# A four-layer metaformer on one core: zero products on TensorE, one broadcast of B written twice, and an accumulation moved behind a scan

## The chip, the cores and the metric

The kernel runs on one core of a Trainium2 chip. The metric is the device time of one execution in microseconds (us), as the median of the executions timed. The engines are called by the profile's names: PE (TensorE, matmuls; PEld is its weight load), DVE (VectorE), ACT (ScalarE), POOL (GpSimd) and SP (SyncE, which here only issues transfers). Each engine works through its own instructions in order and waits on semaphores for the others.

## The reference

The input is x of shape (4, 64, 64, 96). Four layers are applied, each a normalisation over the 96 channels, a mixer and a residual add, and then a small feed-forward block on quantised values with its own residual add. Layer 0's mixer is a gated recurrence. Layers 1 to 3 have a selective scan as mixer, and it is there that the change lies. Cut to what matters, for one direction k, channel d and state n:

```
xs = silu(conv3x3(x @ in_proj))        # 192 channels, 4096 positions, 4 directions
dts, Bs, Cs = split(x_proj @ xs)       # Bs, Cs: 16 states
delta = softplus(dt_proj @ dts + bias)
def step(h, inp):                      # along the 4096 positions
    u_l, dl, b_l, c_l = inp
    dA = exp(dl[..., None] * A)
    h = dA * h + (dl * u_l)[..., None] * b_l[:, :, None, :]
    y = einsum('bkdn,bkn->bkd', h, c_l)
    return (h, y)
y = ys + Ds * u
```

The four directions are added, normalised, gated with silu(z) and projected out.

## The kernel before

Layer 0 is done first for all four images by `gated`. Then `scans` goes through twelve stages, layers 1 to 3 of four images each. A stage has 24 items: two directions `d`, four segments of 1024 positions and three chunks of 128 rows (a row is a channel of one of the two scan orders). An item has 16 tiles, one for each state n. That makes 12 x 24 x 16 = 4608 tiles of 128 x 1024 floats, and the loop takes them in pairs: one step `j` of the loop at the end of `scans` handles tiles a = 2j and b = 2j + 1, so there are 2304 steps.

For a tile k these are the operations, by the helpers' names:

- `decays(k)`: ACT computes da = exp(delta * A).
- `b_rows(k)`: PE spreads row n of B over the 128 rows, by two bf16 matmuls of 512 columns with a matrix `sel` of ones and zeros, into a tile `bc` of PSUM.
- `times_b(k)`: DVE multiplies `bc` in place by `du`.
- `scan(k)`: DVE runs h = da * h + bc along the 1024 positions.
- `c_rows(k)`: SP issues two transfers that spread row n of C into a tile `c` of SBUF (six buffers).
- `times_c(k)`: POOL multiplies h into `c`.
- `accumulate(k)`: PE adds `c` to the open sum `acc` of the item, by four float32 matmuls of 64 x 512 which the profile lists as eight rows. The sum stands open over the 16 tiles.

The tile `bc` comes from `wide()`, which asks a pool of two PSUM buffers for a new tile at each call. With `acc` (two banks) and the two banks of the side work this fills PSUM's eight banks. A buffer is given to a new tile by the scheduler once every instruction that touches the tile before in it has been placed; the new tile's writer then waits for those instructions.

Each engine's instructions stand in the order in which the Python code issues them (the class `InOrder` chains them), so the order written in the loop is the order on the engine. In a step DVE runs `times_b(a)`, `times_b(b)`, `scan(a)`, `scan(b)`. PE runs `accumulate(a - 4)`, `accumulate(b - 4)`, then the side work, then `b_rows(a + 2)` and `b_rows(b + 2)` for the step that follows.

The side work is what lies between two scans: joining directions, the output projection, the feed-forward block, the next layer's input projection and convolution, and preparing the next item's delta. It is written as generators, and `beside` pumps them twice in a step, once after `times_b(a)` and once after `scan(a)`. `pe.columns` counts the columns that PE has been given so far, a float32 column as four; `slot` and the jobs' `share` and `rate` use that count to spread the side work over the steps. At an item's step 6 (`n == 13`) the preparation of the next item is drained to its end, and near the end of a stage the job for the next stage is drained as well.

Of the kernel before, what the change touches and what calls it, by code (L numbers as in the profile page):

```python
# [12 lines left out]
BF16 = mybir.dt.bfloat16  # L13
# [13 lines left out]
MM = 512  # L27
# [10 lines left out]
NB3 = 96  # L38
# [35 lines left out]
    return n / (max(1, 128 // max(rows, 32)) * max(1, 128 // max(cols, 32)))  # L74


PACE = (2.0, 1600), (2.2, 1800), (2.6, 2000)


# [37 lines left out]
def metaformer(ctx: ExitStack, tc: tile.TileContext, x, l0_ab, l0_rest, ssm, ffn, out):  # L117
    nc = tc.nc
    pe, act, dve, pool, sp = (
        InOrder(tc, e) for e in (nc.tensor, nc.scalar, nc.vector, nc.gpsimd, nc.sync)  # L120
    )
# [6 lines left out]
    def sb(bufs, tag, shape, dtype=F32):  # L128
        return pools[bufs].tile(shape, dtype, tag=tag, name=tag)

    def const(name, shape, dtype=F32):
        return pools[1].tile(shape, dtype, name=name)
# [3 lines left out]
    def wide():  # L136
        return wides[0].tile([128, T], F32, tag="bc", name="bc")
# [11 lines left out]
    def settle():  # L149
        banks["free"] += banks["back"]  # L150
        banks["back"] = 0
# [20 lines left out]
    def drain(chain, others=lambda: None, until=lambda: False):  # L172

        while chain is not None and not chain.done and not until():
            if not pump(chain):
                others()
            settle()
# [16 lines left out]
    sel = const("sel", [NB3, NS, 128], BF16)  # L194
    for n in range(NS):
        for k in range(2):
            at = NS * k + n
            dve.tensor_copy(
                sel[:, n, 64 * k : 64 * k + 64], mod32[:, at : at + 1].to_broadcast([NB3, 64])
            )  # L200

    fold = const("fold", [128, 32])
    dve.tensor_tensor(fold, ident[:, 0:32], ident[:, 32:64], ALU.add)
# [9 lines left out]
    for layer in range(4):  # L213
# [8 lines left out]
        b = const(f"b_{layer}", [128, 3 + C])  # L222
# [538 lines left out]
    def slot():  # L761

        load["now"] = max(0, min(load["now"], 4 * load["most"]) - load["most"])
# [102 lines left out]
    def prepare_chunk(item):  # L866

        w, sg = weights[item.layer].w, item.sg
        i = 3 * item.d + item.chunk
        bias = w[:, W_DTB + i : W_DTB + i + 1]  # L870
        f = w[NB3 : NB3 + 2 * R, W_IN + 128 * i : W_IN + 128 * (i + 1)]


        delta, du = sb(2, "delta", [128, T]), sb(2, "du", [128, T])
        for k in range(2):
            cols = slice(k * MM, (k + 1) * MM)
            ps = bank("dt_proj")
            pe.matmul(ps, f, sg.rows[NB3 : NB3 + 2 * R, cols], start=True, stop=True)
            yield
            act.activation(delta[:, cols], ps, AF.Identity, bias=bias)  # L880
            release()
            yield k == 0
        act.activation(delta, delta, AF.Softplus)
        exp_and_ln()
        yield
        yield
        pool.tensor_tensor(du, delta, sg.us[item.chunk], ALU.mult)
        item.delta, item.du = delta, du
# [13 lines left out]
    def scans(stages, jobs, pac):  # L902
# [16 lines left out]
        tiles = [(i, n) for i in items for n in range(NS)]  # L919
        last = len(tiles) - 1  # L920
# [10 lines left out]
        def c_rows(k):  # L931
            i, n = tiles[k]
            c = live[k, "c"] = sb(6, "c", [128, T])
            for half in range(2):
                row = NS * half + n
                sp.dma_start(
                    out=c[64 * half : 64 * half + 64],
                    in_=i.sg.cs[row : row + 1, :].to_broadcast([64, T]),
                )
# [7 lines left out]
        def b_rows(k):  # L947
            i, n = tiles[k]
            b = live[k, "b"] = wide()
            for half in range(2):  # L950
                cols = slice(half * MM, (half + 1) * MM)
                pe.matmul(
                    b[:, cols], sel[:, n, :], i.sg.bs[:, cols], start=True, stop=True
                )
# [31 lines left out]
        def add_quarters(i, v, lhs, start, stop):  # L986

            for k in range(2):
                for j in range(2):
                    p = slice(64 * j, 64 * j + 64)  # L990
                    o = 64 * (j ^ k)
                    pe.matmul(
                        i.acc[o : o + 64, j * MM : (j + 1) * MM],
                        lhs[p],
                        v[p, k * MM : (k + 1) * MM],
                        start=start,
                        stop=stop,
                        tile_position=(64 * j, o),
                    )

        def accumulate(k):
            i, n = tiles[k]
            h = live.pop((k, "c"))
            if n == 0:
                i.acc = pac.tile([128, T], F32, tag="acc", name="acc")
                if i.d == 0:
                    add_quarters(i, i.sg.us[i.chunk], weights[i.layer].skip[:, i.chunk, :], True, False)
                else:
                    add_quarters(i, i.yf, stacked, True, False)
            add_quarters(i, h, stacked, False, n == NS - 1)  # L1010

        def take(i):
            i.y = sb(2, "y", [128, T])
            act.copy(i.y, i.acc)
# [27 lines left out]
        for j in range(len(tiles) // 2 + 2):  # L1042
            q, m = divmod(j, half)
            a, b = 2 * j, 2 * j + 1
            on = b <= last
            if on:
                item = items[q]
                nxt = at(q + 1)
                if m == 0:
                    if q % per == 0:  # L1050
                        item.im.y = dram.tile([3, 128, L], F32, tag="y", name="y")
                        working += jobs[q // per]
                    chain = None
                if m == 2 and nxt is not None:
                    if item.chunk == 2:
                        drain(segment, work, lambda: nxt.sg.steps)
                    chain = Chain(prepare_chunk(nxt), True)
                if item.chunk == 1 and m == 1 and at(q + 2) is not None:
                    if q % per == per - 2:
                        for job in jobs[q // per][:1]:  # L1060
                            while not job.done:
                                job.step()
                                settle()
                    segment = Chain(next_segment(items[q + 2 : q + 5]))
                if m == 4 and nxt is not None:
                    start(nxt)
                    if nxt.d == 1:
                        nxt.yf = sb(2, "y", [128, T])
                        t = slice(nxt.seg * T, (nxt.seg + 1) * T)
                        sp.dma_start(out=nxt.yf, in_=nxt.im.y[nxt.chunk, :, t])  # L1070

            def beside(n):
                slot()
                pumped(chain)
                pumped(segment)
                if n == 13:
                    drain(chain, work)
                    if item.chunk == 2:
                        drain(segment, work)
                work(True)  # L1080
                settle()

            if on:
                decays(b)
            for k in (a - 2, b - 2):
                if 0 <= k <= last:
                    carry(k)
            if a + 2 <= last:
                decays(a + 2)
            if 0 <= b - 2 <= last:  # L1090
                times_c(b - 2)
                del live[a - 2, "h"], live[b - 2, "h"]
            for k in (a - 4, b - 4):
                if 0 <= k <= last:
                    accumulate(k)
                if k + 6 <= last:
                    c_rows(k + 6)
            if on:
                times_b(a)
            beside(2 * m)  # L1100
            if on:
                times_b(b)
                scan(a)
            beside(2 * m + 1)
            if a + 2 <= last:
                b_rows(a + 2)
            if on:
                times_c(a)
                scan(b)
            if b + 2 <= last:  # L1110
                b_rows(b + 2)
            if m == 1 and q >= 1:
                take(items[q - 1])
                store(items[q - 1])
# [241 lines left out]
    with tc.tile_pool(name="pbig", bufs=2, space=bass.MemoryType.PSUM) as wides_pool:  # L1356
# [5 lines left out]
        for at in range(len(stages)):  # L1362
            jobs.append([])
            if at + 1 < len(stages):
                im, layer = stages[at + 1]
                jobs[-1].append(Job(between(im, layer - 1), *PACE[layer > 1]))

            for im in {10: images[:2], 11: images[2:3]}.get(at, ()):
                jobs[-1].append(Job(between(im, 3, im.dst), *PACE[2]))
        with tc.tile_pool(name="pac", bufs=1, space=bass.MemoryType.PSUM) as pac:  # L1370
# [121 lines left out]
```

## Time and profile before

| what | value |
|---|---|
| median of three executions | 19407.92 us (19403.34 to 19430.67) |
| the profiled execution's own time | 19356.33 us |
| its span, first to last instruction | 19354.5 us |
| PE busy | 14811.6 us, 77% |
| ACT busy | 10683.2 us, 55% |
| POOL busy | 13500.1 us, 70% |
| scan, 128x1024, on DVE | 4608 instructions, mean 2331 ns |
| `times_b`, 128x1024, on DVE | 4608 instructions, mean 1216 ns |
| `times_c`, 128x1024, on POOL (other forms among them) | 4992 instructions, mean 2276 ns |
| `accumulate`'s matmuls, rows of 64x512 | 36864 rows, 6192.7 us busy |
| `b_rows`, rows of 96x512 bf16 | 9216 rows, 3171.1 us busy |
| mean granted TensorE clock | 0.823 |

The page counts an engine as busy while one of its instructions runs; matmuls overlap, so a group's busy time is less than rows times mean. "Idle before" in a row is the time that the engine stood idle just ahead of it, and the name behind the arrow is what ended that idle time. The granted clock is the share of TensorE's full clock that it was allowed in a stretch.

### The profile page before, as it was taken

How to read it: one execution, taken by the hardware profiler on the slowest of the kernel's cores; microseconds unless marked ns; L12 is line 12 of the kernel's file. 1: busy time of each engine (PE TensorE's matmuls, PEld its weight loads, DVE VectorE, ACT ScalarE, POOL GpSimd, SP SyncE). 2: the span in 40 equal slices, each digit the busy share in tenths (PEclk: the TensorE clock that was granted, in tenths of full speed). 3: DMA queues.
4: the chain of work that ended last, by engine and by line, in shares of the span. 5: the costliest groups of instructions: out<-in, count | busy, mean ns of one | idle time of the engine just before them, and what ended most of it. 6: DMA issues, size and time to landing. Idle time of an engine off the chain costs nothing.

```text
span 19354.5 us, 236828 instructions
## 1 busy us (share of the span) xinstructions
PE 14811.6 (77%) x75584; PEld 4774.9 (25%) x75584; DVE 17417.6 (90%) x13768; ACT 10683.2 (55%) x17977; POOL 13500.1 (70%) x9220
## 2 busy tenths in 40 slices
PE   8897776776777777777777777777777777777777
PEld 3332121221222222222222222222222222222224
DVE  7668999999999999999999999999999999998994
ACT  3444565565555565565565565565565565565554
POOL 3435777777777777777777777777777777777774
PEclk9898887887887787787887887787887887787876
DMA  2123676676677667667677677667667677677773
GB/s 54 49 60 99 171 189 171 173 189 169 177 191 179 174 179 182 174 180 186 173 181 182 173 182 180 170 180 183 173 180 182 173 180 182 172 182 177 180 179 92
DMA packets 1269928, 3193.12 MB, mean 165 GB/s; under 512 B 440336, under 2 KB 440560, under 8 KB 1262544
## 3 DMA queue, kind: packets, MB, share of 16 engines
q1 hardware_dynamic: 1268688, 3177.97, 64.7%
q8 instruction: 609, 9.98, 0.2%
q14 instruction: 631, 5.17, 0.1%
HBM read 2818.51 MB, written 308.28 MB: 162 GB/s over the span
## 4 chain that ended last, share of the span: by engine, by line
issue 35%; PE 22%; DVE 20%; ACT 6%; DMA 4%; POOL 3%; SPq 1%; POOLq 0%; DVEq 0%; ACTq 0%
DVE h L91 13%; PE acc L91 11%; DVE bc L91 5%; PE bc L91 4%; POOL c L91 2%; PE y_t L91 2%; ACT L91 2%; PE dt_proj L91 1%; DMA c<-cs 1%; ACT da L91 1%; ACT u L91 1%; PE out_proj L91 1%; DVE st L91 1%; SPq L91 1%; DMA u<-u 1%
## 5 line engine op out<-in xcount | busy, mean ns | idle before, releaser
L91 POOL TENSOR_TENSOR c<-h,c 128x1024 f32<-128x1024 f32 (+1 forms) x4992 | 11281.7, 2276 | 4576.5 <-DVE h L91 1847.5
L91 DVE TENSOR_TENSOR_SCAN h<-da,carry,bc 128x1024 f32<-128x1024 f32 x4608 | 10585.8, 2331 | 263.6 <-ACT da L91 205.4
L91 ACT ACTIVATE da<-delta,decay 128x1024 f32<-128x1024 f32 x4608 | 5262.1, 1146 | 2266.5 <-DVE h L91 2256.8
L91 PE MATMUL acc<-c,twice 64*64 64x512 f32 x36864 | 6192.7, 801 | 52.9 <-POOL c L91 52.9
L91 DVE TENSOR_TENSOR bc<-du,bc 128x1024 f32<-128x1024 f32 x4608 | 5475.3, 1216 | 737.2 <-PE bc L91 722.3
L91 PE MATMUL bc<-bs,sel 96*128 96x512 bf16 x9216 | 3171.1, 440 | 3619.7 <-DVE h L91 3518.2
L91 PEld LDWEIGHTS acc<-c,twice 64*64 64x64 f32 x36864 | 1550.1, 172 | 3485.6 <-issue 2661.7
L91 PEld LDWEIGHTS <-sel 96*128 96x128 bf16 x9216 | 639.4, 102 | 5978.4 <-DVE h L91 5470.6
L91 ACT ACTIVATE delta<-dt_proj,w 128x512 f32<-128x512 f32 x576 | 394.4, 685 | 1547.2 <-PE dt_proj L91 1546.0
L91 ACT COPY carry<-h 128x1 f32<-128x1 f32 x3456 | 580.0, 184 | 1080.5 <-DVE h L91 1076.2
L91 ACT ACT_TABLE_LOAD x857 | 1099.5, 1283 | 15.7 <-PEq L1485 0.7
L91 PE MATMUL conv<-pad,taps 64*64 64x256 f32 (+1 forms) x9216 | 781.8, 393 | 42.4 <-ACT u L91 33.3
L91 POOL TENSOR_TENSOR du<-delta,u 128x1024 f32<-128x1024 f32 x288 | 678.3, 2355 | 16.1 <-ACT delta L91 14.6
L91 PE MATMUL x_proj<-u,xp 128*108 128x512 f32 x1152 | 632.3, 660 | 62.3 <-DMA u<-u 34.5
L91 PE MATMUL dt_proj<-rows,w 12*128 12x512 f32 x1152 | 669.7, 662 | 3.7 <-ACT u L91 2.7
L91 ACT ACTIVATE c<-c,l_bias 128x512 f32<-128x512 f32 x384 | 263.8, 687 | 726.8 <-PE c L91 716.8
L91 PEld LDWEIGHTS conv<-pad,taps 64*64 64x64 f32 (+1 forms) x9216 | 430.4, 142 | 600.5 <-issue 387.7
L91 DVE TENSOR_TENSOR_SCAN h<-da,l_carry,bc 128x512 f32<-128x512 f32 x384 | 491.4, 1280 | 41.0 <-DVE bc L91 1.4
L91 POOL CAST hq<-ff_h 128x512 fp8e5<-128x512 f16 x384 | 233.3, 611 | 326.7 <-ACT ff_h L91 326.6
L91 PE MATMUL y_t<-ident,pad 128*128 128x128 f32 (+1 forms) x1536 | 401.8, 348 | 54.2 <-DMA pad<-y 46.8
L91 ACT COPY u<-conv 64x256 f32<-64x256 f32 x768 | 280.6, 365 | 241.7 <-PE conv L91 143.3
L91 PE MATMUL bc<-rows,u 96*128 96x512 f32 x768 | 391.8, 635 | 28.2 <-DVE h L91 27.5
(138 smaller groups left out, 11927.0 us busy)
## 6 DMA issues: line engine op xcount, KB each, us to landing
c<-cs SPq DMA_DIRECT2D x9216, 256.0 KB, 4.5
u<-u SPq DMA_DIRECT2D x288, 512.0 KB, 6.8
y<-y SPq DMA_DIRECT2D x1152, 128.0 KB, 4.2
y<-y SPq DMA_DIRECT2D x144, 512.0 KB, 6.4
xr<-x SPq DMA_DIRECT2D x224, 192.0 KB, 5.3
u<-u SPq DMA_DIRECT2D x288, 128.0 KB, 4.0
pad<-y SPq DMA_DIRECT2D x288, 128.0 KB, 5.8
z<-zl SPq DMA_DIRECT2D x96, 256.0 KB, 4.8
```

Of the source, the lines that this page charges most:

```text
L91: ins = f(*a, **k).ins
```

## The change

Three things are altered in the loop, all on PE and with it one transfer issue on SP:

- `accumulate(b - 4)` and `c_rows(b + 2)` move from the head of the step to a place behind `scan(a)`, the side work and `b_rows(a + 2)`.
- `b_rows(a + 2)` is called twice. Each call takes a new tile from `wide()`; the second takes the entry `live[a + 2, "b"]` over, and `times_b(a + 2)` reads that one. Nothing reads the first.
- Ahead of them `keep_busy` adds up to nine matmuls of 512 columns with `nothing`, a tile of zeros, as stationary operand, into the open sum of tile a - 4's item. Their number is (4608 less the columns that PE was given by the step's side work) / 512.

```diff
+FILL = 4608
...
+    nothing = const("nothing", [NB3, 128], BF16)
+    pool.memset(nothing, 0.0)
...
+        def keep_busy(i, n):
+
+            for j in range(n):
+                pe.matmul(
+                    i.acc[:, j % 2 * MM : (j % 2 + 1) * MM],
+                    nothing,
+                    sel[:, 0 : MM // 128, :],
+                    start=False,
+                    stop=False,
+                )
...
-            for k in (a - 4, b - 4):
-                if 0 <= k <= last:
-                    accumulate(k)
-                if k + 6 <= last:
-                    c_rows(k + 6)
+            if 0 <= a - 4 <= last:
+                accumulate(a - 4)
+            if a + 2 <= last:
+                c_rows(a + 2)
+            before = pe.columns
             if on:
                 times_b(a)
             beside(2 * m)
...
                 times_b(b)
                 scan(a)
             beside(2 * m + 1)
+            if 0 <= a - 4 <= last:
+                keep_busy(tiles[a - 4][0], max(0, FILL - int(pe.columns - before)) // MM)
             if a + 2 <= last:
-                b_rows(a + 2)
+                for _ in range(2):
+                    b_rows(a + 2)
+            if 0 <= b - 4 <= last:
+                accumulate(b - 4)
+            if b + 2 <= last:
+                c_rows(b + 2)
             if on:
                 times_c(a)
                 scan(b)
```

## The prediction

> **What bounds the kernel now.** I read the engines' shares first, then DVE's waits, then the timeline of a step without disturbance. The page's first part:
>
> ```profile
> PE 14811.6 (77%) x75584; PEld 4774.9 (25%) x75584; DVE 17417.6 (90%) x13768; ACT 10683.2 (55%) x17977; POOL 13500.1 (70%) x9220
> ```
>
> DVE is busy 90% of the span, no other engine over 77%. What little DVE waits, by the list of who waited for whom (total us, times, longest):
>
> ```profile
> DVE bc L91 <- PE bc L91: 722.3, 494, 17.9
> ...
> DVE h L91 <- ACT da L91: 205.4, 44, 18.0
> ```
>
> It waits for a broadcast in 494 of 2304 steps, 1.46 us each; in the other 79% PE is in time. One of those, in order of time (start, duration, what; in brackets idle time and its end):
>
> ```profile
> 2821.95 2.33 DVE L91 TENSOR_TENSOR bc<-du,bc 128x1024 f32<-128x1024 f32 x2
> 2822.06 0.19 ACT L91 COPY carry<-h 128x1 f32<-128x1 f32 x1 [1.01 <-DVE h L91]
> 2822.08 0.11 PEld L91 LDWEIGHTS <-sel 96*128 96x128 bf16 x2 [1.71 <-DVE h L91]
> 2822.09 0.61 PE L91 MATMUL bc<-bs,sel 96*128 96x512 bf16 x2 [1.22 <-DVE h L91]
> ...
> 2822.62 1.95 PE L91 MATMUL acc<-c,twice 64*64 64x512 f32 x16
> ...
> 2824.20 4.57 DVE L91 TENSOR_TENSOR_SCAN h<-da,carry,bc 128x1024 f32<-128x1024 f32 x2
> ```
>
> times_b(a) and times_b(b) start 1.13 us apart (2821.95 to 2824.20 for two), two scans follow, and the next pair starts at 2828.69: a step of 6.74 us that DVE alone sets. The broadcast at 2822.09 is tile b's: it waits for the end of scan(b), and times_b(a) covers it. Tile a's was written during scan(b). That half scan of lead is what keeps DVE supplied.
>
> **The second broadcast, and the buffer that it gets.** This decides the case. The first call of b_rows(a + 2) takes the buffer that scan(a) frees; for the second, the built program shows which of the two buffers the scheduler chose. PE's order in one step, with the semaphores waited for:
>
> ```
> Matmult bc_41866<-bs_40331,sel_95 128x512 [waits DVE_49]
> ...
> Ldweights sel_95 [waits DVE_49]
> Matmult bc_41869<-bs_40331,sel_95 128x512 [waits PE_49]
> ...
> Matmult acc_41838<-c_41728,twice_87 64x512 [waits DMAHW6_49,Pool_49]
> ...
> Matmult bc_41882<-bs_40331,sel_95 128x512 [waits PE_49]
> ```
>
> bc_41869, the copy that times_b(a + 2) reads, waits for DVE once more, and the count it waits for is that of scan(b): it was put into b's buffer, and b + 2 (bc_41882) into that of the unread copy. Counted over the program, 1849 of 2303 second copies are so placed ("crossed"); in 454 both copies share a's buffer. A crossed copy can't be written during scan(b). Right behind scan(b) DVE wants times_b(a + 2), so DVE stands still until the copy is there, and PE, in order, holds accumulate(b - 4) and b_rows(b + 2) behind it.
>
> **What a crossed step costs.** No step of the trace waits like this, so I build it from rows for a broadcast that DVE did wait for, at full clock and at half (start of the broadcast, then of times_b):
>
> ```profile
> 8007.72 1.04 PE L91 MATMUL bc<-bs,sel 96*128 96x512 bf16 x4
> 8008.36 1.23 DVE L91 TENSOR_TENSOR bc<-du,bc 128x1024 f32<-128x1024 f32 x1 [1.48 <-PE bc L91]
> ```
>
> ```profile
> 1860.85 1.89 PE L91 MATMUL bc<-bs,sel 96*128 96x512 bf16 x4
> ...
> 1861.92 1.23 DVE L91 TENSOR_TENSOR bc<-du,bc 128x1024 f32<-128x1024 f32 x1 [0.60 <-PE bc L91]
> ```
>
> So 0.64 us at full clock, 1.07 at half. Add 0.13 us, by which the broadcast's weights start after times_b would have (2821.95 to 2822.08): the first stall is 0.77 us, or 1.20.
>
> The second stall is at times_b(b + 2). Its broadcast follows the copy and accumulate(b - 4). At full clock accumulate starts 0.53 us behind the copy's start (2822.09 to 2822.62), takes half of 1.95 = 0.98, and 0.64 later times_b(b + 2) may run: 2.15. times_b(a + 2) started at 0.64 and frees DVE at 1.77. Stall 0.38. At half clock the rows are these:
>
> ```profile
> 8016.18 1.04 PE L91 MATMUL bc<-bs,sel 96*128 96x512 bf16 x2 [2.54 <-DVE h L91]
> ...
> 8017.15 3.69 PE L91 MATMUL acc<-c,twice 64*64 64x512 f32 x16
> ```
>
> 0.97 + 1.85 + 1.07 = 3.89 against 1.07 + 1.13 = 2.20: stall 1.69.
>
> Which clock? The granted clock, by stretches of 3.4 us (PE busy is the first figure after the stretch, the clock comes behind POOL):
>
> ```profile
> 2812.00:2815.40 3.40, 0.66 (x3) 0.17 (x4) 3.40 (x3) 1.30 (x3) 2.70 (x2) 1.00 0.79 213
> 2815.40:2818.80 3.40, 3.40 (x18) 0.94 (x22) 3.40 (x3) 1.64 (x3) 2.46 (x2) 0.53 0.28 70
> ```
>
> PE was busy 0.66 of 3.4 us, and in the next 3.4 us the clock was 0.53. Over the whole trace about a third of the broadcasts that start promptly behind scan(b) run at half clock, and half of the accumulates behind them. The fill evens PE's work out, but a crossed step still has a hole of 1.7 us ahead of every second copy (from the first copy's end to scan(b)'s end; before it was 1.22 to 1.63). I keep these shares: 0.77 + 0.43/3 = 0.91 and 0.38 + 1.31/2 = 1.04, together 1.95 us. Side work of DVE between the two times_b (their starts lie 1.29 us apart on average, not 1.13) hides 0.16: 1.8 us. Bounds: all at full clock 0.77 + 0.38 - 0.16 = 0.99; all at half 1.20 + 1.69 - 0.16 = 2.73.
>
> The Trainium skill ("TensorE: Matmul & The Clock Gate", "HAM oscillation — how this bites in real kernels") says that the clock drops after PE idles for more than about 3.4 us. The trace lost it with holes no longer than 1.7 us. By the rule every crossed step would run warm, and the kernel would end near the low bound below.
>
> **The sum.** 79% of the crossed steps, 1453 or so, have PE in time today: 1453 x 1.8 = 2615 us. In the other 396 PE is late already and sets the step; it gets one broadcast more, 0.45 us (two rows spaced 0.23) to 0.84, I take 0.65: 257 us. The 454 uncrossed steps have copy and accumulate inside scan(b) (0.45 + 0.45 + 0.98 of 2.26 us): nothing.
>
> The fill: 8684 zero matmuls, 3.8 a step and at most 9. No row shows them; the nearest is a broadcast's, 0.23 us, so 1960 us of PE. Nine take 2.03 us. Counted from the second copy's start, PE has done copy, accumulate, broadcast and accumulate(a - 4) at 2.94 and the fill at 4.97; scan(a) ends at 0.64 + 1.13 + 0.38 + 1.13 + 2.26 = 5.54. So the hole ahead of scan(a)'s end hides it. At half clock (3.8 us) the unread copy is late, but still done by scan(b)'s end at 7.80: nothing either way. What it may bring is in the clock, within the bounds above.
>
> accumulate(b - 4), moved, is in the second stall. With it c_rows(b + 2) is issued later on SP, at the latest some 2.5 us into the next step; the page has 4.5 us to landing, and times_c(b + 2) needs it after scan(b + 2), over 7 us into that step. Loads of the side work queue behind it by the same shift and are wanted steps later. Nothing; a POOL delay is covered too, as POOL's two 2.36 us fit a longer step with ease.
>
> A longer step gives ACT's decays more time: of the 205 us above 0 to all may vanish; I take 100. Sum: 2615 + 257 - 100 = +2770 us. The profiled execution ran 19356 us, 52 below the median of 19408; the addition goes onto the median: **22180 us**. Bounds: 1453 x 0.99 + 396 x 0.45 - 205 = +1410, 20820 us; 1453 x 2.73 + 396 x 0.84 = +4300, 23710 us.
>
> **Rivals.**
> - The fill holds the clock at full through the holes. For it: PE is busy 4.97 us of each 7.9 instead of about 3 in a bare step. Against: the hole of 1.7 us sits just ahead of the chain that matters. Then 20,820 us.
> - The clock is lost in nearly every step, since a bare crossed step has two holes (0.6 and 1.7 us) with only a 0.5 us broadcast between. Then 23,400 us or a little more.
> - Not slower: crossing costs nothing, because PE reaches the second copy after scan(b) has ended anyway, and the better clock cuts DVE's 722 us of waits by half. That gives about 19,050. For it: PE is 77% busy. Against: 494 waits only. It decides if under 360 / 1.8 = 200 crossed steps stall, of 1849.
>
> **How the numbers follow.** Forecast 60%, warm rival 23%, cold rival 12%, not slower 5%. The range 20,700 to 23,400 takes in the warm case and most of the cold one. About 0.2% (39 us) is what a measurement of this kernel can tell from no change: faster 0.04, same 0.01, slower 0.95.
>
> **What would show it.** DVE's waits for PE's bc should rise from 494 to over 1800 events and some 3,500 us, with times_b(a) and times_b(b) both waiting; the weights of the second copy should wait for DVE's h in most steps; bare steps should take 7.9 to 9.6 us instead of 6.74. The mean granted clock tells the rivals apart: about 0.8 forecast, 0.95 warm, 0.65 cold. I am wrong if bare steps stay near 6.74 us.

## The result, and the profile after

The changed kernel takes 22114.65 us (median of four, 22068.04 to 22133.45) against 19408.46 us: a ratio of 1.1388 by the means, 95% interval 1.1368 to 1.1409. It is 2706 us slower. The forecast was 22,180.

The engines' shares on the page of the changed kernel, to be put beside those of before:

```profile
PE 18043.5 (82%) x88874; PEld 5448.2 (25%) x88874; DVE 17673.3 (80%) x13768; ACT 10730.2 (49%) x17977; POOL 13488.8 (61%) x9221
```

DVE runs the same 13768 instructions, but its share has fallen from 90% to 80%. PE has 13290 rows more: 8684 zero products and 4606 second broadcasts. What DVE waits for is above all PE's broadcast. In the list of who waited for whom (total us, times, longest), and in the group of `times_b` (busy, mean ns, then idle time before it and what ended it):

```profile
DVE bc L92 <- PE bc L92: 3296.9, 3577, 12.7
```

```profile
L92 DVE TENSOR_TENSOR bc<-du,bc 128x1024 f32<-128x1024 f32 x4608 | 5620.7, 1225 | 3305.9 <-PE bc L92 3296.9
```

The waits were 722.3 us in 494 places and are now 3296.9 us in 3577, while scan and `times_b` themselves last nearly as long as before (2332 ns against 2331, and 1225 against 1216). Of the idle time in this group, 1849 us lie ahead of a step's first `times_b`, 1457 us ahead of the second. One step at full clock, in order of time:

```profile
4350.19 2.32 DVE L92 TENSOR_TENSOR_SCAN h<-da,carry,bc 128x1024 f32<-128x1024 f32 x1
...
4351.37 0.59 PE L92 MATMUL bc<-bs,sel 96*128 96x512 bf16 x2
...
4352.56 0.11 PEld L92 LDWEIGHTS <-sel 96*128 96x128 bf16 x2 [1.09 <-DVE h L92]
4352.57 0.60 PE L92 MATMUL bc<-bs,sel 96*128 96x512 bf16 x2 [0.60 <-DVE h L92]
...
4353.10 1.09 PE L92 MATMUL acc<-c,twice 64*64 64x512 f32 x8
...
4353.21 1.23 DVE L92 TENSOR_TENSOR bc<-du,bc 128x1024 f32<-128x1024 f32 x1 [0.70 <-PE bc L92]
...
4354.12 0.60 PE L92 MATMUL bc<-bs,sel 96*128 96x512 bf16 x2
...
4354.77 1.23 DVE L92 TENSOR_TENSOR bc<-du,bc 128x1024 f32<-128x1024 f32 x1 [0.33 <-PE bc L92]
```

The unread copy is written at 4351.37, during scan(b). The second copy waits for that scan's end (4350.19 + 2.32 = 4352.51) and starts at 4352.57. DVE stands still for 0.70 us, does `times_b(a)`, and stands still again for 0.33 us, because accumulate and then b's broadcast come behind the copy. A step of the same kernel in which both copies share a's buffer:

```profile
6748.68 2.33 DVE L92 TENSOR_TENSOR bc<-du,bc 128x1024 f32<-128x1024 f32 x2
...
6750.93 4.58 DVE L92 TENSOR_TENSOR_SCAN h<-da,carry,bc 128x1024 f32<-128x1024 f32 x2
...
6753.65 1.24 PE L92 MATMUL bc<-bs,sel 96*128 96x512 bf16 x4
...
6754.82 1.09 PE L92 MATMUL acc<-c,twice 64*64 64x512 f32 x8
6755.42 1.21 DVE L92 TENSOR_TENSOR bc<-du,bc 128x1024 f32<-128x1024 f32 x1
```

All four broadcast matmuls run during scan(b), and the next `times_b(a)` starts 6.74 us after this step's, as in a clean step before. Both steps have the same instructions on DVE and the same chain of broadcasts and accumulates on PE. Apart from the side work, what sets them apart is the buffer that the second copy was given.

The span of the profiled executions grew by 2748 us: 71 in layer 0 and 2677 in the scan stages. In the scan stages DVE's idle time ahead of the two `times_b` grew by 2569 us, its busy time by 255, and its other waits fell by 146.

### The profile page after: what moved, and what is told of

The parts are those of the page before. It is cut to its first block, busy times and chain, and to the rows that moved or that the text cites. A ratio compares the mean times of both kernels' runs of the same rounds, so it can differ in the third digit from the quotient of the medians.

```text
span 22102.9 us, 261309 instructions
## 1 busy us (share of the span) xinstructions
PE 18043.5 (82%) x88874; PEld 5448.2 (25%) x88874; DVE 17673.3 (80%) x13768; ACT 10730.2 (49%) x17977; POOL 13488.8 (61%) x9221
## 5 line engine op out<-in xcount | busy, mean ns | idle before, releaser
L92 DVE TENSOR_TENSOR_SCAN h<-da,carry,bc 128x1024 f32<-128x1024 f32 x4608 | 10584.4, 2332 | 202.0 <-ACT da L92 169.0
L92 DVE TENSOR_TENSOR bc<-du,bc 128x1024 f32<-128x1024 f32 x4608 | 5620.7, 1225 | 3305.9 <-PE bc L92 3296.9
L92 PE MATMUL bc<-bs,sel 96*128 96x512 bf16 x13822 | 4770.0, 435 | 3135.3 <-DVE h L92 2923.8
L92 PE MATMUL acc<-c,twice 64*64 64x512 f32 x36864 | 6110.1, 738 | 6.4 <-POOL c L92 6.3
L92 PEld LDWEIGHTS <-sel 96*128 96x128 bf16 x13822 | 996.8, 102 | 7613.7 <-DVE h L92 4377.7
L92 PE MATMUL acc<-sel,nothing 96*128 96x512 bf16 x8684 | 2411.0, 401 | 0.0
L92 PEld LDWEIGHTS acc<-c,twice 64*64 64x64 f32 x36864 | 1117.7, 151 | 2534.7 <-issue 1439.7
L92 PEld LDWEIGHTS <-nothing 96*128 96x128 bf16 x8684 | 794.5, 102 | 1578.3 <-issue 1003.3
L92 ACT COPY y<-acc 128x1024 f32<-128x1024 f32 x288 | 291.5, 1012 | 1566.5 <-PE acc L92 1531.5
```

The costliest lines, as they stand in the source:

```text
L92: ins = f(*a, **k).ins
```

## The experiments

"Crossed" is a step whose second copy was given b's buffer, counted in each built program; in the profiles as many second copies wait for DVE. "First" and "second" are DVE's idle time ahead of a step's first and second `times_b`, from each profile. Ratios are of the means, to the kernel before run beside each version (medians 19410 to 19422 us). e1, e2, e6 and e7 are shown as edits of the changed kernel, the others as edits of the kernel before. All versions but the kernel before have the tile of zeros, which by e8 costs nothing.

| kernel | time us | ratio, 95% interval | crossed | first us | second us | granted clock |
|---|---|---|---|---|---|---|
| before | 19408 | | 0 | 735 | 2 | 0.823 |
| changed | 22115 | 1.1388 (1.1368 to 1.1409) | 1849 | 1849 | 1457 | 0.877 |
| e1, both writes in one tile | 19729 | 1.0154 (1.0133 to 1.0175) | 0 | 755 | 357 | 0.924 |
| e2, no second write | 19632 | 1.0107 (1.0090 to 1.0124) | 0 | 646 | 393 | 0.903 |
| e3, second write alone | 20621, one run | | 1801 | 1937 | 0 | 0.824 |
| e7, no zero products | 21437, one run | | 1083 | 1119 | 1587 | 0.835 |
| e6, accumulate at the end | 21314, one run | | 2064 | 2518 | 0 | 0.865 |
| e4, move alone | 19506 | 1.0045 (1.0030 to 1.0060) | 0 | 374 | 515 | 0.829 |
| e5, zero products alone | 19700 | 1.0153 (1.0139 to 1.0167) | 0 | 1076 | 2 | 0.860 |
| e8, tile of zeros alone | 19421 | 1.0002 (0.9993 to 1.0011) | 0 | 744 | 2 | 0.819 |
| e9, zero products ahead of the side work | 19680 | 1.0143 (1.0124 to 1.0161) | 0 | 1016 | 2 | 0.855 |
| e11, move, zero products ahead | 19490 | 1.0046 (1.0028 to 1.0063) | 0 | 432 | 378 | 0.889 |

### e1: both writes into one tile

```diff
-        def b_rows(k):
+        def b_rows(k, again=False):
             i, n = tiles[k]
-            b = live[k, "b"] = wide()
+            b = live[k, "b"] if again else wide()
+            live[k, "b"] = b
...
-                for _ in range(2):
-                    b_rows(a + 2)
+                b_rows(a + 2)
+                b_rows(a + 2, True)
```

> As the changed kernel, but the second broadcast of tile a + 2 is written into the first one's tile, so that it never takes b's buffer. PE's matmuls are the same in number and order. Theory (the crossed buffer): the wait of every crossed step goes, DVE's waits for PE's bc fall from 3297 us to under 700 us, time 19,000 to 19,500 us. Rival 1 (extra PE work, zero products and second broadcasts, makes PE late): the same work is there, time stays within 300 us of 22,115. Rival 2 (accumulate of b - 4 ahead of b + 2's broadcast is what makes DVE wait): only the wait at times_b(a) goes, the 1457 us at times_b(b) stay, time about 20,700.

The time falls by 2385 of 2706 us with PE's matmuls unchanged. Its line in the list of waits:

```profile
DVE bc L92 <- PE bc L92: 1101.2, 737, 12.6
```

3577 waits have become 737. Rival 1 is out: the same work on PE costs 2385 us less once the second copy may be written during scan(b). The granted clock is higher too, 0.924 against 0.877; e3 shows what crossing costs at the clock of before. Rival 2 is out as the main cause, but it has a point: 357 us at the second `times_b` stay, and the time is 230 us above the range that the theory gave. So 321 us of the loss have another cause than crossing.

### e2: no second write

```diff
-                for _ in range(2):
-                    b_rows(a + 2)
+                b_rows(a + 2)
```

> As the changed kernel, but tile a + 2's broadcast is written once; zero products and the moved accumulate stay. Theory: no step is crossed, time 18,950 to 19,450 us, within 150 us of the kernel with both writes in one tile (4606 broadcast matmuls of 0.23 us less, hidden in a bare step). Rival 1: the zero products are 1960 us of the 3000 us of extra PE work, so at most a third of the loss goes, time over 21,000. Rival 2: about 20,700.

19632 us, 98 us under e1, which is the price of 4606 more broadcast matmuls where they don't cross. The range was missed upwards again (19,450): zero products and the moved accumulate cost about 1% between them.

### e3: the second write alone

```diff
             for k in (a - 4, b - 4):
...
             if a + 2 <= last:
-                b_rows(a + 2)
+                for _ in range(2):
+                    b_rows(a + 2)
```

> As the kernel before, but tile a + 2's broadcast is written twice in two tiles; no zero products, both accumulates at the head of the step. 1801 of 2303 second copies lie in b's buffer. Theory: each crossed step has the wait at times_b(a) of 0.70 us at full clock or 1.15 at half, and none at times_b(b), since no accumulate lies between; with DVE's former waits partly taken in, 1801 x 0.65 to 0.9 = 1170 to 1620 us, time 20,500 to 21,000. Rival 1: second broadcasts are 1040 of 3000 us of PE work, time at most 20,350. Rival 2: time about 19,400.

20621 us, as the theory gave, and 270 us above what the first rival allowed. The group of `times_b`:

```profile
L92 DVE TENSOR_TENSOR bc<-du,bc 128x1024 f32<-128x1024 f32 x4608 | 5473.6, 1223 | 1937.1 <-PE bc L92 1929.6 <-POOL carry L92 7.4
```

All of the 1937.1 us lie ahead of the first `times_b`, none ahead of the second. Each of the 1801 crossed steps waits, the median for 0.70 us; of the 503 others, 29 do. The granted clock is that of before, 0.824 against 0.823, so crossing by itself costs some 1210 us. That is about half of the 2385 us of e1, in which the first wait fell by 1094 us and the second by 1100. The second needs the accumulate between the copy and b's broadcast, as e6 shows.

### e7: without the zero products

```diff
-            if 0 <= a - 4 <= last:
-                keep_busy(tiles[a - 4][0], max(0, FILL - int(pe.columns - before)) // MM)
```

> As the changed kernel, without the zero products. The scheduler then crosses only 1083 of 2303 second copies. Theory: the loss goes with the crossed steps, at 1.45 us net for each (2680 us of the scan stages over 1849 steps), a little more for a lower clock: 1083 x 1.45 to 1.8 = 1570 to 1950 us, time 20,950 to 21,400. Rival 1: the 1960 us of zero products go out of 3000 us of PE work, time about 20,300. Rival 2: the moved accumulate is there in all steps, time about 22,000.

21437 us, 37 us above the theory's range. All of the 1083 crossed steps wait at the first `times_b`, 45 of the other 1221. The second wait is not confined to crossed steps: 1066 us there and 520 us in the others, since the second copy and the accumulate stand ahead of b's broadcast in every step. Without the zero products (1960 us of PE by the forecast's estimate, 2411 us busy in the profile) the kernel is still 2000 us over the one before, so they are not what slows it most. Part of what they do is indirect: without them the scheduler places 1083 copies in b's buffer instead of 1849.

### e6: the accumulate behind b's broadcast

```diff
-            if 0 <= b - 4 <= last:
-                accumulate(b - 4)
-            if b + 2 <= last:
-                c_rows(b + 2)
...
             if b + 2 <= last:
                 b_rows(b + 2)
+            if 0 <= b - 4 <= last:
+                accumulate(b - 4)
+            if b + 2 <= last:
+                c_rows(b + 2)
```

> As the changed kernel, but accumulate(b - 4) and the C rows of b + 2 stand behind b_rows(b + 2), at the step's end. The scheduler crosses 2064 of 2303 second copies. Theory: the wait at times_b(a) stays, 2064 x 0.99 = 2050 us, and the one at times_b(b) falls from 1457 to under 100 us, since nothing but a copy lies ahead of b + 2's broadcast: time 20,500 to 20,950. Rival (both waits come of the crossing itself, wherever the accumulate stands): 2064/1849 of the loss, about 22,400.

The second wait is gone altogether, so it comes of the accumulate between the copy and b's broadcast. The first wait is 2518 us instead of 2050, and the time 21314, over the range:

```profile
L92 DVE TENSOR_TENSOR bc<-du,bc 128x1024 f32<-128x1024 f32 x4608 | 5468.0, 1224 | 2517.7 <-PE bc L92 2510.0 <-POOL carry L92 7.4
```

The median crossed step still waits 0.70 us. The excess lies in steps in which PE is late: the second copy starts over 0.15 us behind scan(b)'s end in 514 crossed steps, with 1269 us of first waits, against 223 steps and 591 us in the changed kernel. That two accumulates then stand together ahead of the zero products would do it, but no run tried that apart.

### e4: the move alone

```diff
-            for k in (a - 4, b - 4):
-                if 0 <= k <= last:
-                    accumulate(k)
-                if k + 6 <= last:
-                    c_rows(k + 6)
+            if 0 <= a - 4 <= last:
+                accumulate(a - 4)
+            if a + 2 <= last:
+                c_rows(a + 2)
...
                 b_rows(a + 2)
+            if 0 <= b - 4 <= last:
+                accumulate(b - 4)
+            if b + 2 <= last:
+                c_rows(b + 2)
```

> As the kernel before, with accumulate(b - 4) and the C rows of b + 2 moved behind b_rows(a + 2); no zero products, one broadcast. Nothing is crossed. Theory: the move takes 0.98 to 1.85 us from ahead of a + 2's broadcast, so waits at times_b(a) fall (735 us to some 400), and it puts it ahead of b + 2's, so waits at times_b(b) appear (2.5 to 400 or 800 us, more than with zero products since the clock is lower): 19,350 to 19,800. Rival (the 210 us that the kernel with zero products and one broadcast lost are the zero products'): no loss here, under 19,400.

As expected: 361 us less at the first `times_b`, 513 more at the second, and 0.45% slower. The accumulate has changed the tile that it delays.

### e5: the zero products alone

```diff
             beside(2 * m + 1)
+            if 0 <= a - 4 <= last and tiles[a - 4][1] != NS - 2:
+                keep_busy(tiles[a - 4][0], max(0, FILL - int(pe.columns - before)) // MM)
```

> As the kernel before, with zero products alone (left out in the one step of eight in which tile b - 4 closes the sum); accumulates at the head of the step, one broadcast. Theory: the clock in the scan stages rises towards 0.9 and no wait is added in steps without much side work; waits at times_b(a) fall or stay, none at times_b(b): 19,150 to 19,450. Rival (zero products push side work and broadcasts back): waits at times_b(a) rise by the 200 to 300 us that the uncrossed kernels lost, 19,600 or more.

The theory fell here. The clock rises to 0.860 and the kernel is 1.53% slower, because DVE waits more:

```profile
DVE bc L92 <- PE bc L92: 1061.5, 601, 19.2
```

Of 7299 zero products the most harm is in steps with three to five: waits ahead of the next `times_b` went there from 162 to 429 us (876 steps). Between the accumulates and the first zero product PE stands idle for 0.70 us on average in those that then wait and 0.05 us in the others, mostly for results of POOL and ACT. That delay the count of columns doesn't see, and the step gets its zero products on top.

### e8: the tile of zeros alone

```diff
+    nothing = const("nothing", [NB3, 128], BF16)
+    pool.memset(nothing, 0.0)
```

> As the kernel before, with the tile of zeros and its memset alone. In the profiles of the changed kernel and of four variants, all with this tile, layer 0 took 40 to 71 us longer than in the one profile of before (first times_b of the scan stages at 1747 to 1779 us against 1708). If the tile is at fault: 19,450 to 19,480 here. If layer 0's time merely differs from run to run with its clock: within 30 us of before.

No difference (0.9993 to 1.0011). Its profile has the first `times_b` of the scan stages at 1767 us, too, so layer 0 most likely differs by such amounts from one execution to another. Only one execution of the kernel before was profiled, which leaves this open.

### e9: zero products ahead of the side work

```diff
+            if 0 <= a - 4 <= last and tiles[a - 4][1] != NS - 2:
+                keep_busy(tiles[a - 4][0], 3)
             if on:
                 times_b(a)
             beside(2 * m)
```

> As the kernel with zero products alone, but three in every step (6048 in all, none where tile b - 4 closes the sum), ahead of the side work instead of behind it. In the kernel with zero products alone, steps that then wait had PE idle some 2.2 to 3.5 us inside their side work ahead of the zero products, other steps 0.8 to 1.0. Theory (the zero products cost because they stand behind side work that itself waits for other engines): ahead of it they fill idle time, waits at times_b(a) go back from 1076 to 650 to 850 us, time 19,300 to 19,550. Rival (they cost as PE work, wherever they stand): waits stay near 1000 us, time 19,600 to 19,700.

The rival holds: 1016 us of waits at the first `times_b`, 1.43% slower. Idle time of PE inside the side work doesn't take the zero products up, although they now stand ahead of it. There was little of it: the 2.2 to 3.5 us that the theory started from are PE's idle time since a's broadcast one step earlier, so they take in its wait for scan(b) ahead of b's broadcast (1.69 of 2.46 us in the steps of e5 with three to five zero products that then wait). The zero products cost as work of PE between two broadcasts, and the explanation in e5 by their place is not the whole of it.

### e11: the move with zero products ahead of the side work

```diff
+            if 0 <= a - 4 <= last:
+                keep_busy(tiles[a - 4][0], 3)
             if on:
                 times_b(a)
             beside(2 * m)
...
+            if 0 <= b - 4 <= last:
+                accumulate(b - 4)
```

> As the kernel with the moved accumulate alone, with three zero products in every step (6912) ahead of the side work; one broadcast. Theory: the higher clock shortens the accumulate that stands ahead of b + 2's broadcast, waits at times_b(b) fall from 515 to 300 to 400 us, those at times_b(a) stay at 350 to 450: 19,350 to 19,500, no clear gain on the kernel before. Rival (zero products cost as PE work): waits at times_b(a) rise by 200 us or more, 19,650 or more.

All three numbers fall into the theory's ranges: 432 us first, 378 second (515 without zero products), 19490 us. With the accumulate out of the way zero products have room ahead of a's broadcast (they add 58 us to the first wait, where they added 281 in e9), and the second wait falls with the better clock, 0.889 against 0.829; the sum is no gain, 1.0046 against 1.0045 for the move alone. None of the versions beats the kernel before.

## Why the prediction was right

**The crossed buffer, right.** That 1849 second copies wait for scan(b) was read off the built program; every one of these 1849 steps shows a first wait, and 3 of the other 455. Taking the crossing away (e1) takes 2385 of the 2706 us, which is 88%.

**The size of a crossed step, right.** The first stall at full clock was put at 0.77 us, between the start that `times_b` would have had and the one it gets. The profile says 0.70 of idle time; the other 0.07 is about the overlap of scan and `times_b` (0.08 us in a clean step before: 2824.20 + 4.57 against 2828.69), which a wait breaks up. (DVE's busy time in the scan stages rose by 255 us; 41 of them are `times_b`'s longer mean, 9 ns on each of 4608; 214 remain for 3583 breaks against 513 before, 0.07 each.) The second stall was put at 0.38 us and is 0.33 and a break of 0.07, so 0.40. At half clock a step like this was expected:

```profile
8687.92 1.02 PE L92 MATMUL bc<-bs,sel 96*128 96x512 bf16 x2 [1.68 <-DVE h L92]
...
8688.86 1.99 PE L92 MATMUL acc<-c,twice 64*64 64x512 f32 x8
8688.97 1.23 DVE L92 TENSOR_TENSOR bc<-du,bc 128x1024 f32<-128x1024 f32 x1 [1.11 <-PE bc L92]
...
8691.70 1.23 DVE L92 TENSOR_TENSOR bc<-du,bc 128x1024 f32<-128x1024 f32 x1 [1.50 <-PE bc L92]
```

With a break each they are 1.18 and 1.57 us, against the 1.20 and 1.69 of the forecast: within a tenth.

**The clock, half right.** The forecast kept the shares of before, a third of the copies and half of the accumulates at half clock. The second holds: 48% of the accumulates in that place take over 1.2 us. The first does not: 13% of the broadcasts that start promptly behind scan(b), against 32% before. The clock rose to 0.877 (0.835 without the zero products, e7) where about 0.8 was forecast. Yet PE still stands idle for 1.63 us (median) ahead of these broadcasts, and the accumulates behind them often run at half clock. In e1, with the same matmuls, PE's idle time ahead of the broadcast behind scan(b) is 0.18 us (median), and 2% of those broadcasts run at half clock. The two rivals with an all-warm and an all-cold chain are both out by the time and by these shares; the mean clock alone would have left the warm one (0.95) about as near as the forecast.

**The sum, term by term.** Of the crossed steps 1378 had PE in time before, where 1453 were assumed. They gained 1.66 us of idle time each, and 0.13 us of broken overlap (the second break in 92% of the crossed steps): 1.79 against the 1.8 of the forecast, 2467 us against 2615. That 1.79 is so near 1.8 is luck, as two errors cancel. With the measured shares the forecast's terms give 0.83 + 1.01 - 0.16 = 1.68 us, and the 1280 of these steps whose second copy starts right behind scan(b) (within 0.15 us of its end) cost about that: 1.54 us of idle time and the broken overlap. In the other 98 PE comes late, and they gained 3.25 us of idle time each, which the sum did not have. The other 471 gained 0.73 us and one break, 0.80 against 0.65: 377 against 257. The steps that were not crossed were put at nothing; in 42 of them PE had been late before, and they lost 2.1 us of waits each, 90 us in all. DVE's other waits fell by 146, where 100 were taken off. The 71 us in layer 0 were not forecast and are most likely no work of the change: e8's profile, with layer 0 at about the same time, belongs to a kernel that is no slower.

**What was wrong: "the hole ahead of scan(a)'s end hides it".** The fill and the moved accumulate were costed at nothing outside crossed steps, by the time line of a step without side work. Without any crossing they cost 1.07% (e2), and the fill alone 1.53% (e5). Only 395 of 2304 steps got six zero products or more, so a step with little side work is the exception. In 1017 of the 2233 steps that have zero products, the last of them ends over 0.15 us behind the end of scan(a), which was to hide them. That these 200 to 300 us don't show in the total is in part luck: the 98 late steps made up for a clock that was better than forecast. How much of them falls into waits of crossed steps that were priced anyway, no run shows.

**"Not slower" needed under 200 crossed steps to stall.** All 1849 did.

## What to carry to other kernels

A tile asked for from a pool is a claim on a buffer: asking twice for something of which one copy is read can take a buffer from the tile that overlaps with it, and which step is hurt is decided by the scheduler's placing, so read the waits in the built program, not the loop. In a pipeline with two buffers the lead of one engine over the other is the whole of its slack, and whatever stands between two writes of that engine, useful or not, is paid for where the slack is already used. Work that is added to keep a clock up must be measured against the waits that it makes: here the clock rose in each kernel with zero products and none of them was faster.

## What the runs showed of the hardware

- A wait of DVE costs more than its idle time: a scan and the `times_b` behind it overlap by 0.08 us in a clean step, and a wait between them takes that overlap away (214 us of busy time for 3070 more breaks, 0.07 us each).
- Matmuls with zeros as stationary operand raise the granted clock: alone they took it from 0.823 to 0.860 (e5), and with the moved accumulate from 0.829 to 0.889 (e4 and e11).
- The two waits did not follow the clock alike. With zero products the second fell (515 to 378 us, e4 to e11), and the first rose (735 to 1076, before to e5), although a broadcast is faster at full clock (its two rows take 0.60 us against 1.02 in the steps shown).
